# A deformable convolution layer: two of the eight corner weights of a tap move from ScalarE to GpSimd

## The chip, the cores and the metric

The kernel runs on one core of a Trainium2 chip. The core has five engines that work side by side, each through its own queue in order: TensorE (PE, with the weight loads shown apart as PEld), VectorE (DVE), ScalarE (ACT), GpSimd (POOL) and SyncE (SP, which here only issues DMAs). The metric is the time on the device, in microseconds (us), as the median over runs; less is better.

## The reference, cut to what matters

Four layers follow each other on x, an array of 4 images of 128 channels and 128 x 128 pixels, with a group normalisation before and an addition after each: a deformable convolution, a factored dilated convolution, a state space layer with four scans over the image, and a 3 x 3 convolution. The change touches the deformable convolution alone. For each output pixel and each of nine taps an offset is computed from the image, the image is sampled at that fractional position, and a weight matrix is applied:

```python
return corner(y0i, x0i, (1 - ly) * (1 - lx)) + corner(y0i, x0i + 1, (1 - ly) * lx) + corner(y0i + 1, x0i, ly * (1 - lx)) + corner(y0i + 1, x0i + 1, ly * lx)
...
sampled = _bilinear_sample(x, py, px) * mask[:, None]
return jnp.einsum('bckhw,ock->bohw', sampled, weight.reshape(weight.shape[0], C, KK))
```

So a sample is a sum of four corners, each with a weight of its own for every pixel. The first two corners (row `y0`) are called the upper neighbours here, the other two the lower.

## The kernel before, in words

**The main thread and what runs beside it.** The function `scan` writes out the state space layer's four scans, 512 blocks of 16 scan instructions (L1073) on VectorE. Everything else, the deformable layer of the next image included, is written as Python generators that are advanced between scan instructions; `together` sets how far the side work has come for each share of the scans. The order in which the generators are advanced is the order of the instructions on every engine, and `keep_order` makes it final. So when one engine is late, the others find their own work behind the wait that this causes. The first image's deformable layer runs with no scan beside it.

**Which engine does the scan's products.** While a deformable layer runs, the side work announces that GpSimd is busy. The scan then multiplies its states with the output factors on VectorE (L997, the DVE form) instead of GpSimd, and all four input products of a block (L930) are on VectorE as well. GpSimd keeps one 128 x 512 product per block in that time (L902, `steps`), which waits for a copy on ScalarE (L899).

**The deformable layer** (`layer0`). An image has 32 blocks of 4 rows (512 pixels); a block has nine taps, so there are 288 taps in an image and 1152 in all. A table in device memory holds for every position the four corners side by side, 4 x 128 values. A tap goes through these steps:

- `gather` (L447): four indirect DMAs on GpSimd's queue, one for each row of 128 pixels. Rows come in pairs: pair `h` (0 or 1) fills one tile `g` of 128 partitions x 2 rows (`r`) x 4 corners (`c`) x 128 channels. The pool of these tiles has 20 buffers (10 taps) for the first image and 10 buffers (5 taps) for the other three.
- `weigh_upper(h)` (L460): on ScalarE, one instruction on 128 x 128 for each row and upper corner, four for a pair, eight for a tap.
- `weigh_lower(h)` (L473): on VectorE, both lower corners of both rows of a pair in one instruction; its weights `wl` lie in PSUM.
- `turn` (L484): 16 transposing matmuls on TensorE, which add up the four corners in PSUM.
- `copy` (L496, ScalarE), `project` (L504, TensorE, two matmuls), and after the ninth tap `add` (L511, VectorE).

Every 36 taps `positions` works out the indices and weights of the next strip of 16 rows, mostly on VectorE (the indices `idx` at L417).

**The order of a tap's steps** is the list that `weave` reads. Each entry is a delay in taps and a function; at step `t` each function is called for tap `t` less its delay:

```python
order = [[(2, weigh_upper(0)), (2, weigh_lower(0)), (3, turn), (5, project)], [(6, add), (0, gather), (4, copy(True))],
         [(2, weigh_upper(1)), (2, weigh_lower(1))], [(0, look), (3, copy(False))], []]
```

So at one step GpSimd issues the gathers of tap `t`, ScalarE and VectorE weigh tap `t - 2`, and TensorE turns tap `t - 3`. A gather waits until the buffer that it fills is free, that is until the tap five (in the first image ten) before it has been turned.

Of the kernel before, what the change touches and what calls it, by code (L numbers as in the profile page):

```python
# [13 lines left out]
AF = mybir.ActivationFunctionType  # L14
ALU = mybir.AluOpType
# [9 lines left out]
NBLK = H // R  # L25
KK = 9
# [86 lines left out]
def conv_preact_kernel(ctx: ExitStack, tc: tile.TileContext, a: dict, nb: int):  # L113
    nc = tc.nc
# [8 lines left out]
    def load(pool, src, shape, name, **kw):  # L123
        t = pool.tile(shape, F32, name=name, **kw)
        nc.sync.dma_start(t, src)
        return t
# [75 lines left out]
    def blk(t, i):  # L202
        return t[:, i * N : (i + 1) * N]
# [108 lines left out]
    def layer0(st, pairs=10):  # L312
# [5 lines left out]
        with ExitStack() as s:  # L318
# [8 lines left out]
            got = {}  # L327
# [106 lines left out]
            def where(n):  # L434
                i, k = divmod(n, KK)
                return i, k, i // BPS, i % BPS

            def gather(n):
                i, k, j, q = where(n)
                if k == 0:  # L440
                    got["x", i] = load(pp, blk(xb, i), [P, N], "xres", bufs=2)
                idx = got["i", j][1]
                for h in range(2):
                    got["g", n, h] = g = gp.tile([P, 2, 4, P], F32, name="g")
                    for r in range(2):
                        m = ((2 * h + r) * BPS + q) * KK + k
                        nc.gpsimd.indirect_dma_start(  # L447
                            out=g[:, r].rearrange("p q c -> p (q c)"),
                            out_offset=None,
                            in_=table,  # L450
                            in_offset=bass.IndirectOffsetOnAxis(ap=idx[:, m : m + 1], axis=0),
                        )

            def weigh_upper(h):
                def one(n):
                    i, k, j, q = where(n)
                    wv, g = got["i", j][0], got["g", n, h]
                    for r in range(2):
                        for c in range(2):
                            nc.scalar.activation(  # L460
                                g[:, r, c, :], g[:, r, c, :], AF.Copy, scale=wv[:, 2 * h + r, q, k, c : c + 1]
                            )

                return one

# [72 lines left out]
            for n, _ in enumerate(positions(0)):  # L538
                yield share * min(1.0, (n + 1) / 21)
            order = [[(2, weigh_upper(0)), (2, weigh_lower(0)), (3, turn), (5, project)], [(6, add), (0, gather), (4, copy(True))],  # L540
                     [(2, weigh_upper(1)), (2, weigh_lower(1))], [(0, look), (3, copy(False))], []]
            while st["rows"] <= NBLK:
# [841 lines left out]
    def head(b):  # L1384
        st = sts[b]
        table = [(loads(None, layer0_table(st), True), 12)] if b < 2 else []
        return table + [(loads("POOL", layer0(st)), 28), (loads("PE", layer1(st), True), 14),
                (loads("PE", layer2_pre(st), True), 36)]
# [11 lines left out]
    for f in layer0(sts[0], 20):  # L1400
        tick()
        for _ in range(3):
            next(ahead, None)
            tick()
# [103 lines left out]
```

## Time and profile before

| | |
|---|---|
| median of 3 runs | 20775.48 us (20770.23 to 20790.63) |
| the profiled execution, its own time | 20873.01 us, 0.47% above that median |
| its span, first to last instruction | 20871.2 us |
| busy DVE / POOL / PE / ACT | 16828.5 / 15930.9 / 15906.6 / 13184.7 us |
| indirect gathers L447 on POOL | 4608, mean 1043 ns, busy 4807.6 us |
| upper weights L460 on ACT | 9216, mean 392 ns, busy 2897.4 us |
| first image's gathers (stage A) | from 215 to 1933 us of the span, no scan beside |
| second, third, fourth image's (stages B, C, D) | 3449 to 5328, 8650 to 10450, 13548 to 15369 us, with scans |

How to read the profile: all times count from the first instruction of the span. A row of a group gives line, engine, operation, what it writes and reads, and the count; behind the bar its busy time in us and the mean ns of one; behind the second bar the idle time of the engine just before these instructions, and who ended most of it. "issue" means that nothing the profile shows was waited for. Busy time of neighbouring instructions can overlap, so that 9216 instructions of 392 ns fill 2897.4 us, not 3613.

### The profile page before, as it was taken

To read this page: it belongs to the slowest core of one execution; us is meant where nothing else is said; L and a number is where in the kernel's file an instruction comes from. 1 tells how busy PE (TensorE), PEld (TensorE's weight loads), DVE (VectorE), ACT (ScalarE), POOL (GpSimd) and SP (SyncE) were. 2 spreads that over 40 slices of the span, in tenths; PEclk is the share of its full clock that TensorE was granted. 3 is DMA by queue.
4 is the path that set the end of the run, shared out by engine and by line. 5 is a ranking of instruction groups with operands and counts; after the bars stand their busy time and mean duration, and the time that the engine had idled before them with its cause. 6 is when DMAs were issued, how large, how long until landed. Compare 5 with 4: busy or idle time off the path is not lost.

```text
span 20871.2 us, 208527 instructions
## 1 busy us (share of the span) xinstructions
PE 15906.6 (76%) x58778; PEld 6786.0 (33%) x58778; DVE 16828.5 (81%) x14665; ACT 13184.7 (63%) x26230; POOL 15930.9 (76%) x9453
## 2 busy tenths in 40 slices
PE   4667776777878888777788887877777877677778
PEld 2444222444322223344422222344432222222223
DVE  1222588888999999878799889978889998999983
ACT  3444566677666666666667776666666767655563
POOL 3664577666788888777668888866768889999994
PEclk7878888889989999889889999988888988899899
DMA  7666678777767777777777796777776777555673
GB/s 234 191 193 190 193 228 284 248 255 252 246 206 226 231 237 254 236 253 255 247 232 226 224 249 230 255 240 246 252 237 218 235 215 220 185 185 193 199 219 120
DMA packets 2909344, 4717.42 MB, mean 226 GB/s; under 512 B 1095248, under 2 KB 1369240, under 8 KB 2831264
## 3 DMA queue, kind: packets, MB, share of 16 engines
q1 hardware_dynamic: 2539552, 3495.83, 52.3%
q0 software_dynamic: 368640, 1208.25, 18.5%
q8 instruction: 476, 7.80, 0.1%
q14 instruction: 676, 5.54, 0.1%
HBM read 3766.27 MB, written 908.60 MB: 224 GB/s over the span
## 4 chain that ended last, share of the span: by engine, by line
DVE 35%; PE 21%; issue 11%; ACT 11%; DMA 9%; another core or an unknown queue 5%; POOL 3%; SPq 3%; DVEq 0%; POOLq 0%; ACTq 0%
DVE h L1073 20%; DVE h L930 11%; PE pst L484 5%; PE psum L895 4%; DMA du<-stepsd 3%; ACT pa L960 3%; ACT g L460 3%; PE acc L504 2%; DVE g L473 2%; PE dub L923 2%; DMA delta<-stepsd 2%; PE yacc L971 2%; PE p L1303 1%; DMA g<-table,idx 1%
## 5 line engine op out<-in xcount | busy, mean ns | idle before, releaser
L1073 DVE TENSOR_TENSOR_SCAN h<-pa,carry,h 128x512 f32<-128x512 f32 x8192 | 10010.0, 1268 | 811.5 <-ACT pa L960 582.9
L960 ACT ACTIVATE pa<-delta,neg_a 128x512 f32<-128x512 f32 x8192 | 5535.9, 686 | 4528.0 <-DVE h L1073 3464.9
L997 POOL TENSOR_TENSOR h<-h,cb 128x2048 f32<-128x2048 f32 x1692 | 7670.8, 4534 | 136.3 <-POOL carry L991 0.4
L447 POOL DMA_INDIRECT g<-table,idx x4608 | 4807.6, 1043 | 2454.1 <-issue 1523.6
L930 DVE TENSOR_TENSOR h<-du,dub 128x2048 f32<-128x2048 f32 x1625 | 3688.0, 2270 | 961.8 <-PE dub L923 294.7
L484 PE MATMUL pst<-ident,g 128*128 128x128 f32 x18432 | 2693.6, 303 | 1242.6 <-issue 516.0
L923 PE MATMUL dub<-u,xb_sb 128*128 128x512 f32 x3250 | 2073.1, 724 | 1843.3 <-DVE h L930 1532.3
L484 PEld LDWEIGHTS pst<-ident,g 128*128 128x128 f32 x18432 | 2377.9, 158 | 2230.3 <-issue 1139.0
L460 ACT ACTIVATE g<-g,wt 128x128 f32<-128x128 f32 x9216 | 2897.4, 392 | 50.8 <-DMA g<-table,idx 47.6
L971 PE MATMUL yacc<-h,gather_sb 128*32 128x512 f32 x16384 | 2375.6, 644 | 108.9 <-POOL h L997 63.8
L930 POOL TENSOR_TENSOR h<-du,bb 128x2048 f32<-128x2048 f32 x423 | 1927.7, 4557 | 16.5 <-DMA du<-stepsd 16.5
L496 ACT COPY smp<-pst 128x512 f32<-128x512 f32 x1152 | 664.7, 577 | 1749.8 <-remote 1175.9
L473 DVE TENSOR_TENSOR g<-g,wl 128x512 f32<-128x512 f32 x2304 | 1485.7, 671 | 194.3 <-issue 108.5
L504 PE MATMUL acc<-smp,w_sb 128*128 128x512 f32 x2304 | 1355.3, 670 | 307.7 <-DVE x L511 162.8
L923 PEld LDWEIGHTS dub<-u,xb_sb 128*128 128x128 f32 x3250 | 600.3, 213 | 3025.2 <-DVE h L930 2200.9
L902 POOL TENSOR_TENSOR steps<-steps,u 128x512 f32<-128x512 f32 x512 | 652.9, 1275 | 1095.3 <-ACT steps L899 1080.0
L1303 PE MATMUL p<-xn,w_l_sb 128*128 128x508 f32 (+2 forms) x2304 | 1148.6, 620 | 1.8 <-ACT xn L1282 1.8
L971 PEld LDWEIGHTS yacc<-h,gather_sb 128*32 128x32 f32 x16384 | 343.5, 111 | 1886.3 <-issue 1349.6
L895 PE MATMUL psum<-e,ident 128*128 128x512 f32 x1024 | 607.1, 677 | 387.7 <-ACT bc L889 348.5
L511 DVE TENSOR_TENSOR x<-acc,xres 128x512 f32<-128x512 f32 x128 | 87.5, 684 | 967.5 <-remote 500.4
L895 PE MATMUL psum<-one_e,less 128*128 128x512 f32 x1024 | 629.2, 701 | 297.3 <-ACT one_e L891 296.5
L997 DVE TENSOR_TENSOR h<-h,cb 128x2048 f32<-128x2048 f32 x356 | 816.6, 2294 | 12.1
(169 smaller groups left out, 17288.9 us busy)
## 6 DMA issues: line engine op xcount, KB each, us to landing
cb<-bcd SPq DMA_DIRECT2D x512, 1024.0 KB
delta<-stepsd SPq DMA_DIRECT2D x2048, 256.0 KB
du<-stepsd SPq DMA_DIRECT2D x2048, 256.0 KB
stepsd<-steps SPq DMA_DIRECT2D x512, 512.0 KB
table<-gt SPq DMA_DIRECT2D x512, 256.0 KB
bb<-bcd SPq DMA_DIRECT2D x512, 256.0 KB
win<-nd SPq DMA_DIRECT2D x512, 160.0 KB
g<-table,idx POOLq DMA_INDIRECT x4608
```

The costliest lines, as they stand in the source:

```text
L447: nc.gpsimd.indirect_dma_start(out=g[:, r].rearrange("p q c -> p (q c)"), out_offset=None, in_=table, in_offset=bass.IndirectOffsetOnAxis( ...
L460: nc.scalar.activation(g[:, r, c, :], g[:, r, c, :], AF.Copy, scale=wv[:, 2 * h + r, q, k, c : c + 1])
L473: nc.vector.tensor_mul(g, g, wl.unsqueeze(3).to_broadcast([P, 2, 2, P]))
L484: nc.tensor.matmul(pst[:, r * P : (r + 1) * P], g[:, r % 2, q, :], ident, start=q == 0, stop=q == 3, is_transpose=True,)
L504: nc.tensor.matmul(got["a", i], w0[:, k, :], got.pop(("c", n)), start=k == 0, stop=k == KK - 1)
L895: nc.tensor.matmul(pd, sign, t, start=n == 0, stop=n == 3)
L923: nc.tensor.matmul(p, xb[:, seq[t][1], j, :], c["u"], start=True, stop=True)
L930: engine.tensor_mul(h, c["du"], b.unsqueeze(1).to_broadcast([P, NG, N]))
L960: nc.scalar.activation(pa, blocks[t]["d", g], AF.Exp, scale=neg_a[:, k, at : at + 1])
L971: nc.tensor.matmul(c["y"][g * Q : (g + 1) * Q, :], gather, c["h", j][:, g, :], start=j == 0, stop=last and not second,)
L997: engine.tensor_mul(h, h, c["cb"][:, j, :].unsqueeze(1).to_broadcast([P, NG, N]))
L1073: nc.vector.tensor_tensor_scan(o, f, o, carry[:, n : n + 1], ALU.mult, ALU.add)
```

## The change

In `gather`, behind the two indirect DMAs of a pair, GpSimd now multiplies one slice of an older tile: row 1, upper corner 1 of the same pair of the tap two before. ScalarE leaves that slice out. For the last two taps of an image, which no later gather follows, ScalarE does it as before. A small function `neighbour` returns the slice and the column of its weights.

```diff
                             in_offset=bass.IndirectOffsetOnAxis(ap=idx[:, m : m + 1], axis=0),
                         )
+                    if n >= 2:
+                        g, w = neighbour(n - 2, h, 1, 1)
+                        nc.gpsimd.tensor_scalar(g, g, w, None, ALU.mult)
+
+            def neighbour(n, h, r, c):
+                i, k, j, q = where(n)
+                return got["g", n, h][:, r, c, :], got["i", j][0][:, 2 * h + r, q, k, c : c + 1]
 
             def weigh_upper(h):
                 def one(n):
-                    i, k, j, q = where(n)
-                    wv, g = got["i", j][0], got["g", n, h]
                     for r in range(2):
                         for c in range(2):
-                            nc.scalar.activation(
-                                g[:, r, c, :], g[:, r, c, :], AF.Copy, scale=wv[:, 2 * h + r, q, k, c : c + 1]
-                            )
+                            if r == 1 and c == 1 and n + 2 < NBLK * KK:
+                                continue
+                            g, w = neighbour(n, h, r, c)
+                            nc.scalar.activation(g, g, AF.Copy, scale=w)
 
                 return one
```

## The prediction

> **What bounds the kernel now.** I began with the page's busy shares and slices.
>
> ```profile
> PE 15906.6 (76%) x58778; PEld 6786.0 (33%) x58778; DVE 16828.5 (81%) x14665; ACT 13184.7 (63%) x26230; POOL 15930.9 (76%) x9453
> ...
> ACT  3444566677666666666667776666666767655563
> POOL 3664577666788888777668888866768889999994
> ```
>
> No engine is full over the whole span, and ACT, which the change relieves, is the least busy of the four. The change acts in four stages only, so next comes the view that sums busy time by stretch, one row for each image's gathers (A, B, C, D).
>
> ```profile
> core 0: us, PE busy (x) PEld busy (x) DVE busy (x) ACT busy (x) POOL busy (x), PEclk, DMA share, GB/s
> 215.00:1933.00 1718.00, 1027.82 (x5584) 739.58 (x5585) 431.75 (x751) 819.54 (x2544) 1092.56 (x1152) 0.79 0.64 191
> 3449.00:5328.00 1879.00, 1466.84 (x7298) 823.19 (x7297) 1624.06 (x1646) 1297.91 (x3361) 1278.93 (x1184) 0.89 0.75 251
> 8650.00:10450.00 1800.00, 1370.82 (x6979) 797.55 (x6980) 1416.38 (x1488) 1207.83 (x3210) 1268.62 (x1178) 0.88 0.76 248
> 13548.00:15369.00 1821.00, 1369.97 (x6968) 795.96 (x6968) 1416.11 (x1486) 1208.36 (x3210) 1274.69 (x1178) 0.87 0.75 245
> ```
>
> By busy time POOL looks two thirds full (1274.7 of 1821 in D). The timeline of POOL in stage B, and of VectorE beside it, says otherwise:
>
> ```profile
> 4371.64 0.95 POOL L447 DMA_INDIRECT g<-table,idx  x1 [0.30 <-issue]
> 4374.77 0.95 POOL L447 DMA_INDIRECT g<-table,idx  x1 [2.19 <-ACT smp L496]
> 4376.02 0.95 POOL L447 DMA_INDIRECT g<-table,idx  x1 [0.30 <-issue]
> 4377.15 1.28 POOL L902 TENSOR_TENSOR steps<-steps,u 128x512 f32<-128x512 f32 x1 [0.18 <-ACT steps L899]
> 4378.58 0.98 POOL L447 DMA_INDIRECT g<-table,idx  x1
> ```
>
> ```profile
> 4372.35 2.29 DVE L997 TENSOR_TENSOR h<-h,cb 128x2048 f32<-128x2048 f32 x1
> ```
>
> Two things are to be seen. A gather shows 0.95 us but the next starts 1.25 us later: 0.30 us belong to it and to nothing that is waited for. And the gap of 2.19 us spans VectorE's L997 to 0.13 us past its end (4374.64): ScalarE's copy is named, but the gather was held by that product. So POOL's occupied time is busy time, plus 0.30 us for each of 1152 gathers (346 us), plus the gaps over an L997 (read off the timeline: 0, 121, 30 and 28 us). That makes 1438 of 1718 us in A, 1746 of 1879 in B, 1644 of 1800 in C and 1649 of 1821 in D. In B to D POOL is the fullest engine (91 to 93%); VectorE has 86, 79 and 78%. The stage's first gather also waits about 30 us for its indices (34.5, 30 and 31). What is left for POOL to give is 280, 98, 126 and 141 us.
>
> Last, the chain of waits in stages A and B:
>
> ```profile
> by line: another core or an unknown queue 37.3%; PE pst L484 16.8%; ACT g L460 13.8%; issue 12.2%; PE acc L504 7.9%; ACT smp L496 2.6%; DVE g L473 2.5%; POOL g L447 2.2%; DMA g<-table,idx 2.0%; PE po L359 1.3%; DVE x L511 0.3%; PE ptp L366
> by line: issue 20.8%; DVE h L1073 10.1%; PE pst L484 9.3%; DVE h L930 8.0%; DVE g L473 7.5%; ACT g L460 7.1%; another core or an unknown queue 6.3%; DMA g<-table,idx 4.3%; PE acc L504 4.1%; PE dub L923 3.2%; ACT pa L960 2.6%; POOL g L447 2.
> ```
>
> The upper weights L460 are 13.8% of the chain in A and 7.1% in B (5.9 and 6.3% in C and D). No single engine carries it.
>
> **The change, part by part.**
>
> *Removed from ACT.* Each image loses 286 x 2 = 572 of 2304 weighings. Eight take 2.45 us in a row, 0.306 us each: 175 us of ACT per image. On the path lies at most a quarter of L460's share of the chain: 1718 x 13.8% / 4 = 59 us in A, 33, 27 and 29 us in B, C, D. Where POOL sets the pace none of it counts, so I take it in A alone.
>
> *Added to POOL.* 572 multiplications of 128 x 128 by a column, per image. The trace has no such instruction. Its rows give a line: L997 on POOL, 2048 elements, 4534 ns; L902, 512 elements, 1275 ns; so 2.12 ns an element and 189 ns fixed, and L991, a copy of 4 elements, takes 195 ns as the line says. At 128 elements that is 0.46 us. L902 stood between two gathers at the cost of 4378.58 - 4376.02 - 1.25 = 1.31 us, of which 0.18 was a wait: 0.15 us less than its own 1.28, because it takes over part of the 0.30. So one scale costs POOL 0.46 - 0.15 = 0.31 us, an image 572 x 0.31 = 177 us. Lower end: L991's 195 ns, 0.05 us net, 26 us an image. Upper end: L902 itself, 1.28 us, 645 us an image; but it reads two tensors four times as long, so for the range I use the line plus the fixed part once more for the column of weights, 0.65 us: 0.50 net, 286 us an image. I take the middle because it lies on the line of three rows.
>
> The Trainium skill ("GPSIMD Engine Reference", section 4.1) speaks against the change: plain elementwise work belongs on VectorE, and GpSimd is about half as fast with two inputs, which L997 confirms (4534 against 2294 ns). The same row calls GpSimd roughly line-rate with one input. By that and its 1.2 GHz, as an estimate, a scale would take 0.107 + 0.189 = 0.30 us, net 0.15, and an image 86 us; no run here shows it.
>
> *Waits that move.* The scale waits for gathers issued two taps earlier, at least eight gathers or 10 us. Each gather ends with 16 packets of 4 bytes; their order gives landing at a median of 3.3 us after issue in A and 4.0 to 4.2 in B to D, 99% within 8.6. So that wait is nothing; were it not, the next pair's gathers would queue behind it. The pair h = 1 now stands behind the scale of h = 0 in POOL's queue, and L902 behind both. No DMA and nothing on SP moves. TensorE's turn now also waits for POOL, for a scale behind the gathers of two taps on. Counting gathers issued when a turn starts, POOL is 8.0 taps ahead in A and 3.5 to 3.75 in B to D (medians); three are needed, and 4% or fewer have less. A turn that waits holds TensorE's scan products behind it and VectorE behind those.
>
> *The shared path with VectorE.* L997 holds gathers already, as seen; the scales wait in the same 2.3 us, not in new ones. The other way round, a scale is running 2 x 0.46 / 6.4 = 14% of the time and would hold L997 for 0.23 us on average: 334 x 0.14 x 0.23 = 11 us in all, which I leave out.
>
> The skill ("SBUF — State Buffer", section "Who interferes with whom") says a VectorE instruction with two SBUF inputs contends with a GpSimd instruction that reads SBUF, but infers that such a tensor_tensor leaves descriptor generation alone. The gap of 2.19 us disagrees for these indexed gathers. By the inference POOL would have had 121 us more to give in B; the sum goes by the gap.
>
> *Sum.* Of what POOL has left, I let the scales use half, since the rest is tied to waits at fixed places (L902 for L899, strip ends). B: 177 - 49 = 128. C: 177 - 63 = 114. D: 177 - 71 = 106. A: 177 - 140 - 59 = -22; but there TensorE's hold-ups in "an unknown queue" set the pace, which I can't price, so I take 0, between -59 and +177. Sum 348 us. The profiled execution would go from 20873 to 21221; carried over to the median, 0.47% lower, 20775 + 348 = 21123, rounded 21120 (+1.7%).
>
> **The rivals.**
>
> *1. GpSimd has room, ACT's relief counts (faster).* Speaks for it: gathers wait for ACT by name, POOL's busy time is 76%. Against: most of those gaps lie over L997 or are the 0.30 us. It decides if a scale's net cost is under 98/572 = 0.17 us in B, 0.22 in C, 0.25 in D, that is under some 0.32 us of duration. Then the quarters of L460 are the gain: 59 + 33 + 27 + 29 = 148 us, 20627.
>
> *2. The scale is dear.* At 0.65 us: 286 less the same halves, 237 + 223 + 215 = 675, and in A 286 - 140 - 59 = 87. Sum 762, 21540. For it: the column operand, which no row has.
>
> *3. A new wait takes over.* Once POOL sets the pace, ACT, VectorE and TensorE catch up, and turns stand at the three-tap limit waiting for the scale. If one turn in ten then waits for half a tap of gathers (2.5 us), that is 29 x 2.5 = 72 us a stage, 215 in three, on top of the forecast: 21340. Against: a turn is due two taps (10 us) before its buffer is wanted.
>
> *4. Nothing moves:* only if a scale's cost equals what POOL has left.
>
> **How the numbers follow.** The forecast has 0.47 (21000 to 21260), rival 1 0.16, rival 2 0.17, rival 3 0.15, rival 4 0.05. About 0.2% (42 us) is what a measurement of this kernel tells from no change. Of rival 1 some 0.03 falls within it: faster 0.13, same 0.08, slower 0.79. The range leaves out most of rival 1 and rival 2's end: 20700 to 21500.
>
> **What would show it.** A new POOL row, 2288 scales, near 0.46 us; L460 at 6928. POOL's occupied share in B to D at 97% or more, the stages at about 2000, 1910 and 1925 us, A near 1718. Under rival 1 the stages shrink and POOL stays near 95%; under rival 3 "PE pst L484 <- POOL g" stands among the longest waits. I am wrong if the scale's row is far from 0.46, if its own wait is on a DMA, or if stage A moves by more than 100 us.

## The result, and the profile after

The changed kernel takes 21419.07 us (median of 4 runs, 21407.09 to 21436.96) against 20772.85 us before on the same chip: a ratio of 1.0306, 95% interval 1.0294 to 1.0318. That is 646 us slower, where the forecast had 348 us. 21419 lies within its range of 20700 to 21500, though outside the 21000 to 21260 to which it gave its chance of 0.47. The profiled execution of the changed kernel has a span of 21435.2 us and is compared with the span of before, 20871.2 us: 564 us more.

In the changed file the gather is still L447; the new product on GpSimd is L455, ScalarE's weighing L468 (was L460), VectorE's L479, the turn L490, ScalarE's copy L502, GpSimd's `steps` L908 and the product by the output factors L1003 (was L997). The page of the changed kernel, busy shares and slices, answers to the first view shown of before:

```profile
PE 16207.9 (76%) x58778; PEld 6768.2 (32%) x58778; DVE 16921.0 (79%) x14665; ACT 12642.1 (59%) x23942; POOL 17673.4 (82%) x11741
...
ACT  3444565555667766555566776655556767665563
POOL 4886577888788888888878888888878889999994
```

ScalarE lost 543 us of busy time, GpSimd gained 1743. The stretches of the four stages (their gathers, as before; same columns):

```profile
215.00:2001.00 1786.00, 1171.68 (x5671) 751.64 (x5671) 486.13 (x763) 717.87 (x2027) 1490.88 (x1723) 0.83 0.63 184
3511.00:5551.00 2040.00, 1524.21 (x7314) 825.87 (x7313) 1650.23 (x1655) 1152.05 (x2806) 1746.65 (x1755) 0.87 0.72 232
8862.00:10859.00 1997.00, 1447.98 (x7011) 794.45 (x7011) 1443.38 (x1497) 1082.03 (x2666) 1703.81 (x1749) 0.87 0.71 225
13947.00:15947.00 2000.00, 1443.96 (x7011) 793.87 (x7011) 1445.51 (x1500) 1081.70 (x2665) 1706.31 (x1750) 0.87 0.71 224
```

From first gather to last, A is 66 us longer (1784 against 1718), B 161 (2040 against 1879), C 198 and D 178: 603 us, where the two spans differ by 564: the whole loss lies in these four stages. POOL's timeline in stage D shows what fills them:

```profile
15005.67 0.62 POOL L455 TENSOR_SCALAR g<-g,wt 128x128 f32<-128x128 f32 x1
15006.46 1.01 POOL L447 DMA_INDIRECT g<-table,idx  x1 [0.17 <-POOL g L455]
15007.78 0.94 POOL L447 DMA_INDIRECT g<-table,idx  x1 [0.30 <-PE acc L510]
15008.75 0.63 POOL L455 TENSOR_SCALAR g<-g,wt 128x128 f32<-128x128 f32 x1
15009.56 1.01 POOL L447 DMA_INDIRECT g<-table,idx  x1 [0.17 <-POOL g L455]
```

The gap between two gathers is 0.30 us as it always was, 0.17 us behind a scale and 0.03 us ahead of one. Behind the stage's first gather no gap of POOL is longer than 0.34 us in any of the four stages. Before, longer gaps held 269, 241, 176 and 192 us beyond their first 0.34 us each; this sum is called POOL's waiting from here on. POOL is now occupied from end to end. A pair of gathers with its scale takes 3.10 us from start to start (median of 2200), a pair without one 2.50 us in before (median of 4432): a scale costs 0.60 us of POOL, 343 us in an image.

The groups of POOL and ACT, first as they were before (L447 and L460), then in the changed kernel:

```profile
L447 POOL DMA_INDIRECT g<-table,idx x4608 | 4807.6, 1043 | 2454.1 <-issue 1523.6 <-DMA xres<-in_x_dram 214.2 <-ACT smp L496 175.7
L460 ACT ACTIVATE g<-g,wt 128x128 f32<-128x128 f32 x9216 | 2897.4, 392 | 50.8 <-DMA g<-table,idx 47.6
```

```profile
L447 POOL DMA_INDIRECT g<-table,idx x4608 | 4949.3, 1074 | 1409.3 <-issue 496.7 <-POOL g L455 350.0 <-DMA xres<-in_x_dram 215.4
...
L455 POOL TENSOR_SCALAR g<-g,wt 128x128 f32<-128x128 f32 x2288 | 1597.6, 698 | 77.3
```

```profile
L468 ACT ACTIVATE g<-g,wt 128x128 f32<-128x128 f32 x6928 | 2295.3, 393 | 659.4 <-DMA g<-table,idx 617.1 <-issue 27.5 <-POOL g L455 6.8
```

The waits of the changed kernel (what waits, for what, us in total, times, longest us):

```profile
PEld pst L490 <- POOL g L455: 2412.1, 1442, 7.3
...
PE pst L490 <- POOL g L455: 2044.1, 1339, 6.9
DVE g L479 <- DMA g<-table,idx: 1590.7, 775, 7.2
```

The scale takes 0.62 us (median 622 ns; the mean of 698 holds 86 long ones of 1.8 us and more, all of them over a VectorE L1003). No group of idle time on POOL is put down to the scale's own wait for data. Everything downstream now waits for POOL: ScalarE and VectorE for gathers that have not landed, TensorE's turn for the scale.

### The profile page after: what moved, and what is told of

The parts are those of the page before. It is cut to its first block, busy times and chain, and to the rows that moved or that the text cites. A ratio compares the mean times of both kernels' runs of the same rounds, so it can differ in the third digit from the quotient of the medians.

```text
span 21435.2 us, 211218 instructions
## 1 busy us (share of the span) xinstructions
PE 16207.9 (76%) x58778; PEld 6768.2 (32%) x58778; DVE 16921.0 (79%) x14665; ACT 12642.1 (59%) x23942; POOL 17673.4 (82%) x11741
## 5 line engine op out<-in xcount | busy, mean ns | idle before, releaser
L1003 POOL TENSOR_TENSOR h<-h,cb 128x2048 f32<-128x2048 f32 x1692 | 7674.2, 4536 | 136.9 <-POOL carry L997 1.0
L447 POOL DMA_INDIRECT g<-table,idx x4608 | 4949.3, 1074 | 1409.3 <-issue 496.7
L490 PE MATMUL pst<-ident,g 128*128 128x128 f32 x18432 | 2901.8, 304 | 2126.7 <-POOL g L455 2044.1
L490 PEld LDWEIGHTS pst<-ident,g 128*128 128x128 f32 x18432 | 2311.9, 156 | 3415.8 <-POOL g L455 2412.1
L479 DVE TENSOR_TENSOR g<-g,wl 128x512 f32<-128x512 f32 x2304 | 1533.1, 674 | 1778.9 <-DMA g<-table,idx 1590.7
L468 ACT ACTIVATE g<-g,wt 128x128 f32<-128x128 f32 x6928 | 2295.3, 393 | 659.4 <-DMA g<-table,idx 617.1
L455 POOL TENSOR_SCALAR g<-g,wt 128x128 f32<-128x128 f32 x2288 | 1597.6, 698 | 77.3
L502 ACT COPY smp<-pst 128x512 f32<-128x512 f32 x1152 | 668.7, 581 | 1569.9 <-PE acc L510 1449.1
L510 PE MATMUL acc<-smp,w_sb 128*128 128x512 f32 x2304 | 1491.1, 735 | 25.4 <-DVE x L517 24.4
L908 POOL TENSOR_TENSOR steps<-steps,u 128x512 f32<-128x512 f32 x512 | 653.7, 1277 | 906.6 <-ACT steps L905 904.6
L1003 DVE TENSOR_TENSOR h<-h,cb 128x2048 f32<-128x2048 f32 x356 | 821.3, 2307 | 12.2
```

What stands on the lines that cost most here:

```text
L447: nc.gpsimd.indirect_dma_start(out=g[:, r].rearrange("p q c -> p (q c)"), out_offset=None, in_=table, in_offset=bass.IndirectOffsetOnAxis( ...
L455: nc.gpsimd.tensor_scalar(g, g, w, None, ALU.mult)
L468: nc.scalar.activation(g, g, AF.Copy, scale=w)
L479: nc.vector.tensor_mul(g, g, wl.unsqueeze(3).to_broadcast([P, 2, 2, P]))
L490: nc.tensor.matmul(pst[:, r * P : (r + 1) * P], g[:, r % 2, q, :], ident, start=q == 0, stop=q == 3, is_transpose=True,)
L510: nc.tensor.matmul(got["a", i], w0[:, k, :], got.pop(("c", n)), start=k == 0, stop=k == KK - 1)
```

## The experiments

The first theory after the result: **POOL's time** is the loss. A stage takes its old length or POOL's occupied time, whichever is longer, and 572 scales of 0.60 us net push the occupied time over the old length. The rival: **the new wait**. TensorE's turn waits 2412 us for POOL's scale in the view above, and that chain (gather two taps on, scale, turn) sets the pace. A second question is why the scale costs what it does, and a third what ScalarE's relief is worth. Runs of one group share one chip and the runs of the kernel before on it: 20858.91 us for the spare tile, the corner left out, the one pair and the buffers; 20769.86 for the three quarters, the wait alone (two kernels) and the prices; 20782.94 for the form of two tiles, where it fits and the one pair run again. The last run had a chip of its own. In the kernels with a scratch tile the lines are shifted by one or a few.

**The scale on a tile that nobody reads.**

```diff
-                        nc.gpsimd.tensor_scalar(g, g, w, None, ALU.mult)
+                        nc.gpsimd.tensor_scalar(spare, ident, w, None, ALU.mult)
...
-                            if r == 1 and c == 1 and n + 2 < NBLK * KK:
-                                continue
```

> ScalarE weighs all eight upper corners again; GpSimd does the same 2288 multiplications, behind the same gathers and with the same column of weights, but from a constant into a scratch tile that nothing reads. So GpSimd's time stays and the wait for its result is gone. Theory 1 (GpSimd's own time is the loss: 0.60 us for each multiplication, 343 us an image, GpSimd without a pause in all four stages): about the changed kernel's 21419 us, between 21350 and 21500, and GpSimd again without waits. Theory 2 (the wait of TensorE's turn for GpSimd, three taps instead of five, is the loss): near the 20773 us of the kernel before, at most 20900.

Measured: 21393.95 us, ratio 1.0262 (1.0245 to 1.0279). The turns have nothing to wait for on POOL, and most of the loss is there. In us it is 25 below the changed kernel's first runs; the ratio is lower because the kernel before is slower on this chip. Its stages are 1782, 2031, 1989 and 1988 us, within 12 us of the changed kernel's, with no idle time on POOL.

**The corner left out.**

```diff
-                    if n >= 2:
-                        g, w = neighbour(n - 2, h, 1, 1)
-                        nc.gpsimd.tensor_scalar(g, g, w, None, ALU.mult)
```

> One upper corner of each pair is left out altogether: ScalarE weighs three, GpSimd none (the last two taps of an image as before). Theory 1: ScalarE's relief is worth little where GpSimd is the fullest engine: 20700 to 20780 us. Rival (ScalarE's share of the chain counts): a quarter of that share in the four stages, 148 us, 20625 us or less.

Measured: 20814.3 us, 0.9981 (0.9972 to 0.9991). ScalarE's relief by itself is worth 45 us, little more than two chips differ by (see the one pair below): its stages are 1710, 1864, 1800 and 1799 us against 1718, 1879, 1799 and 1821.

**One pair only.**

```diff
-                    if n >= 2:
+                    if n >= 2 and h == 1:
...
-                            if r == 1 and c == 1 and n + 2 < NBLK * KK:
+                            if h == 1 and r == 1 and c == 1 and n + 2 < NBLK * KK:
```

> Only the second pair of a tap has its corner weighed on GpSimd, 286 an image instead of 572; ScalarE does the first pair's. Theory 1: GpSimd gets 172 us an image. What it had left in the four stages was 280, 98, 126 and 141 us, so the first image's stage stays, and the other three grow by 74, 46 and 31 us: 20925 us, between 20850 and 21000. Theory 2 (any wait for GpSimd brings the three-tap limit): most of the 646 us are back, 21200 or more.

Measured: 20824.56 us, 0.9983 (0.9973 to 0.9992). Half of the scales cost nothing, where a proportional cost would have been 320 us. POOL's waiting has gone from 269, 241, 176 and 192 us to 88, 0, 8 and 6: the scales used the whole of the room in B to D. My rule that only half of it could be used is wrong. The expected 20925 missed too, though it let the scales use all of the 98, 126 and 141 us that I had reckoned for B to D: there was more room than that. The kernel stands at the edge.

The same kernel was run again later on another chip:

> The kernel in which GpSimd weighs the corner of the second pair alone, once more in five rounds, beside the kernel before: whether half of the products is really a little faster, or the same. GpSimd is filled and no more in the last three stages, so both theories: 0.997 to 1.000.

Measured: 20784.16 us, 1.0000 (0.9991 to 1.0009). So the gain of the first time isn't a property of the kernel that can be relied on; between two chips the ratio moved by 0.17%, and the relief of 0.19% above is no surer than that.

**Fewer buffers in the first image.**

```diff
-        layer0(sts[0], 20)
+        layer0(sts[0], 10)
```

> The kernel before, with 10 instead of 20 buffers for the first image's gathered tiles, nothing else. In the kernel before, ScalarE's copy waited 1176 us in all for something that the profile does not name, in stage A above all, with gathers up to ten taps ahead; in the changed kernel, whose gathers keep about two and a half taps ahead of the turns, that wait is gone. Theory a (the hold-ups come from gathers that run far ahead): stage A goes from 1718 us towards the 1440 us of the gathers alone, 20500 to 20700 us. Theory b (the hold-ups have another cause and the buffers only bridge them): stage A is the same or longer, 20770 to 20950 us.

Measured, on the kernel before with this edit: 20858.41 us, 1.0003 (0.9994 to 1.0013). In before, some of ScalarE's copies start long after the transposes that they read have ended (in stage A 90 of 288, by a median of 9.8 us), and the trace names what released them only as "remote". Halving the buffers left it as it was: 693 us in stage A before, 728 in this kernel. For the whole span (before, then this kernel):

```profile
ACT smp L496 <- remote: 1175.9, 219, 34.3
```

```profile
ACT smp L496 <- remote: 1210.3, 213, 17.6
```

In the changed kernel no wait of this kind is left, on any engine. What it is was not found; it doesn't depend on these buffers.

**Three quarters of the scales**, to see whether the cost sets in at the edge.

```diff
-                    if n >= 2:
+                    if n >= 2 and (h == 1 or n % 2 == 0):
```

(The condition of ScalarE's `continue` changes with it.)

> GpSimd weighs the corner for both pairs in every second tap and for the second pair alone in the others: 429 scales an image, where the change has 572 and the kernel with one pair has 286. If GpSimd's occupied time bounds a stage as soon as its idle time is used up, and the kernel with one pair stands just at that point, the stages are those of the changed kernel less 143 times 0.60 to 0.65 us: some 1695 in the first, which then stays at before's 1718, and 1950, 1910 and 1910 in the others, together 270 us over before, ratio 1.013. If each scale costs the same wherever it stands, three quarters of the change's loss: 480 us, 1.023. If what costs is something that sets in only with the last scales (the turns that wait for GpSimd in every tap), under 1.005.

Measured: 21049.07 us, 1.0134 (1.0118 to 1.0151), the first theory's 1.013. The stages by gathers were expected at 1718, 1950, 1910 and 1910 us and came out at 1698, 1947, 1902 and 1902.

```profile
218.00:1915.00 1697.00, 1125.13 (x5671) 737.10 (x5671) 483.51 (x762) 759.38 (x2168) 1389.81 (x1580) 0.84 0.67 193
3415.00:5362.00 1947.00, 1466.02 (x7314) 800.52 (x7313) 1644.27 (x1653) 1191.49 (x2949) 1639.73 (x1613) 0.90 0.76 243
8666.00:10567.00 1901.00, 1393.78 (x7011) 779.88 (x7011) 1444.99 (x1497) 1116.23 (x2806) 1593.58 (x1606) 0.88 0.74 236
13660.00:15561.00 1901.00, 1392.01 (x7011) 778.71 (x7011) 1442.43 (x1498) 1115.50 (x2801) 1593.71 (x1606) 0.89 0.75 236
```

Each row loses 101 to 113 us of POOL's busy time against the changed kernel's, and 89 to 99 us of its length, where 143 scales of 0.60 us are 86: where POOL is the bound, the stage follows it.

**The wait alone.** The changed kernel and one that differs only in whose data the scale touches, side by side. In the second nobody weighs that corner.

```diff
-                        nc.gpsimd.tensor_scalar(g, g, w, None, ALU.mult)
+                        nc.gpsimd.tensor_scalar(spare, ident, w, None, ALU.mult)
```

> GpSimd does its product from the identity into a scratch tile that nobody reads, ScalarE weighs the other three, and nobody weighs that one corner: the work on each engine is the change's, without the wait of the transposes for GpSimd's product. If the wait costs nothing, the ratio is the changed kernel's, 1.031 within 0.002. If it costs what the changed kernel had over the scratch tile with all eight on ScalarE, 1.026 or less.

> The changed kernel itself, so that it stands beside the others against the same runs of the kernel before. Both theories: 1.031 within 0.002.

Measured: 21393.25 us, 1.0302 (1.0285 to 1.0319) without the wait; 21413.23 us, 1.0308 (1.0291 to 1.0325) with it. The difference of 0.0006, 20 us between the medians, is within either interval. So the turn's wait is not what the 643 us are made of. Without it other waits took its place (waits of the kernel without the scale's wait):

```profile
ACT g L469 <- DMA g<-table,idx: 2658.9, 2465, 23.8
DVE g L480 <- DMA g<-table,idx: 2438.9, 1250, 8.1
```

All of them are waits for the same late engine: POOL issues gathers as fast as it can, and what hangs on a gather waits, whichever semaphore comes last.

**What a product costs on GpSimd.** ScalarE weighs all eight; behind each pair one of four forms goes into the scratch tile, by tap.

```diff
+                        if n % 4 == 0:
+                            nc.gpsimd.tensor_scalar(spare, ident, w, None, ALU.mult)
+                        elif n % 4 == 1:
+                            nc.gpsimd.tensor_scalar(spare[:, 0:64], ident[:, 0:64], w, None, ALU.mult)
+                        elif n % 4 == 2:
+                            nc.gpsimd.tensor_scalar(spare, ident, 0.5, None, ALU.mult)
+                        else:
+                            nc.gpsimd.tensor_copy(spare, ident)
```

> ScalarE weighs all eight neighbours again. Behind each pair of gathers GpSimd runs one instruction from the identity into a scratch tile that nobody reads, its form going round with the tap: the product with a column on 128 elements, the same on 64, the product with a constant on 128, a plain copy on 128. If the scale's 0.62 us is the price of reading its factor from a column, the form with a constant and the copy take about 0.46 us, the row of three rows. If it is the price of f32 elements on this engine, all three forms on 128 take about 0.62 and the one on 64 elements between 0.31 (nothing fixed) and 0.46 (half of it fixed). The time follows the mean price: with the means of 0.62, 0.40, 0.46 and 0.46, 0.14 us less per instruction than the change's own form, 78 us a stage that GpSimd fills, so near 1.015 of before; with 0.62, 0.40, 0.62 and 0.62, near 1.022.

Measured: 21035.39 us (one run), 1.013 of before. The four forms among POOL's groups:

```profile
L457 POOL TENSOR_SCALAR spare<-ident,wt 128x128 f32<-128x128 f32 x568 | 432.3, 761 | 22.0
L461 POOL TENSOR_SCALAR spare<-ident 128x128 f32<-128x128 f32 x576 | 370.6, 643 | 15.4
...
L459 POOL TENSOR_SCALAR spare<-ident,wt 128x64 f32<-128x64 f32 x568 | 324.9, 572 | 18.7
L463 POOL COPY spare<-ident 128x128 f32<-128x128 f32 x576 | 218.8, 380 | 2.7
```

The means hold the instructions that were stopped beside VectorE; the medians are 622, 558, 463 and 297 ns. Neither expectation was right. The column costs 64 ns, not 160. The two widths give 2.5 ns an element and some 304 ns fixed for the form with a scalar, against 2.12 and 189 on my line; the copy takes less than half. So it is the form of the instruction that sets the price.

**The same product in the form that the line was drawn through.** My line went through two products of two tiles, L997 and L902, and L991, a copy of four elements, lay on it.

```diff
-                        nc.gpsimd.tensor_scalar(g, g, w, None, ALU.mult)
+                        nc.gpsimd.tensor_mul(g, g, w.to_broadcast([P, P]))
```

> The change with its product written as a product of two tiles, the weight's column broadcast along the row, in place of the product with a scalar column. The three rows that the forecast drew its line through were products of two tiles (4534 ns for 2048 elements, 1275 for 512); if the line holds for that form at 128 elements, the new rows show 0.46 us instead of the 0.62 of the change, 0.16 us less for each of 572 in four images, 92 us a stage while GpSimd stays filled: about 1.0308 less 366 of 20770, so 1.013. If a short product costs what the scalar form does, 1.031. If reading two operands or the broadcast costs more on short rows, above 1.031. The turns wait for GpSimd here as in the change.

Measured: 20842.81 us, 1.0032 (1.0020 to 1.0044). The same work in another form takes back nine tenths of the loss. The product's row (duration min/median/max) and its timeline in stage D:

```profile
L455 POOL TENSOR_TENSOR g<-g,wt x2288: 407/409/2552, 229.0 to 15360.9; 128x128 f32<-128x128 f32 x191
```

```profile
15002.57 0.42 POOL L455 TENSOR_TENSOR g<-g,wt 128x128 f32<-128x128 f32 x1
15003.14 0.98 POOL L447 DMA_INDIRECT g<-table,idx  x1 [0.16 <-POOL g L455]
15004.43 0.95 POOL L447 DMA_INDIRECT g<-table,idx  x1 [0.30 <-issue]
15005.40 0.41 POOL L455 TENSOR_TENSOR g<-g,wt 128x128 f32<-128x128 f32 x1
```

0.41 us, a little under the line's 0.46, and 2.83 us for a pair with it: 0.33 us net, the forecast's 0.31. It did better than the expected 1.013 because that sum took off 0.16 us a product, where the net price fell by 0.27. The stages are 1686, 1876, 1839 and 1836 us, with 45, 0, 1 and 1 us of waiting on POOL: full, and hardly over the edge.

**Where it fits.** The form of two tiles, for the second pair alone, and in the first image, whose stage had most room, for the first pair of every second tap as well.

```diff
-                    if n >= 2:
+                    if n >= 2 and (h == 1 or pairs == 20 and n % 2 == 0):
...
-                            if r == 1 and c == 1 and n + 2 < NBLK * KK:
+                            if (h == 1 or pairs == 20 and n % 2 == 0) and r == 1 and c == 1 and n + 2 < NBLK * KK:
```

> GpSimd weighs the corner of the second pair alone, and in the first image, whose stage had the most idle time, also of the first pair in every second tap; written as a product of two tiles. If a product costs 0.46 us, GpSimd has some 45 us left in each stage of the last three images, and the first stage takes 1690 to 1700: 20 to 60 us less than before, 0.997 to 0.999. If it costs 0.62 or more, the stages of the kernel with one pair and the first stage of the one with three quarters: 0.998 to 1.000, and above 1.000 only if the product costs over 0.65.

Measured: 20709.61 us, 0.9967 (0.9957 to 0.9978), in the same group as the two runs of 1.0000 and 1.0032. By the ratios it beats the kernel before by 0.33% and the changed one by 3.3%. POOL keeps 98, 52, 36 and 40 us of waiting in stages of 1693, 1829, 1764 and 1775 us. All four are shorter than those of the kernel without the corner, in which ScalarE is relieved of more and POOL of everything; that run was on another chip, but it raises the question of what the gain comes from.

**Relief, or a slower pace of gathers?** The same products at the same places on the scratch tile, with ScalarE weighing all eight.

```diff
-                        nc.gpsimd.tensor_mul(g, g, w.to_broadcast([P, P]))
+                        nc.gpsimd.tensor_mul(spare, ident, w.to_broadcast([P, P]))
```

> The same products at the same places as where they fit (second pair, and in the first image every second tap's first pair), but from the identity into a scratch tile that nobody reads, with ScalarE weighing all eight neighbours. If the 0.33% of the kernel where they fit comes from ScalarE's relief, it is gone: 1.000 to 1.002, since GpSimd still has some 40 us of idle time a stage. If it comes from the gathers' slower pace (a product between two pairs spreads them), it stays: 0.996 to 0.998.

Measured: 20453.56 us against 20081.66 us of the kernel before, 1.0182 (1.0168 to 1.0196). Neither expectation holds, and the run doesn't answer the question, for it went to a chip on which the kernel before is over 3% faster than on the others (its granted clock is 0.904 there, 0.889 on the chip of the run above). Its stretches:

```profile
216.00:1797.00 1581.00, 1066.98 (x5694) 698.42 (x5694) 482.64 (x762) 920.82 (x2597) 1284.71 (x1581) 0.88 0.70 208
3303.00:5096.00 1793.00, 1424.62 (x7322) 812.34 (x7321) 1653.17 (x1656) 1307.35 (x3381) 1472.27 (x1470) 0.90 0.79 264
8405.00:10146.00 1741.00, 1357.16 (x7016) 787.31 (x7016) 1445.40 (x1497) 1232.80 (x3229) 1424.96 (x1463) 0.89 0.79 257
13231.00:14969.00 1738.00, 1360.58 (x7016) 787.69 (x7016) 1447.64 (x1498) 1233.85 (x3228) 1422.34 (x1463) 0.89 0.79 258
```

The products are the same and cost the same (409 to 412 ns), but POOL has 0, 6, 2 and 1 us of waiting, and the stages are as long as its occupied time. By the net price of 0.33 us the added products come to 429 x 0.33 + 3 x 286 x 0.33 = 425 us; 372 were measured. That fits a kernel before in which, on that chip, POOL had next to no room: the room that the others had would then be time in which TensorE was held up. There is no profile of before from that chip, so this is argued and not shown, and whether the gain where it fits comes from ScalarE or from the pace stays open.

## Why the prediction was right, and where it was wrong

**POOL sets the pace: right.** The prediction's occupied times, read as busy time plus 0.30 us a gather plus the gaps over L997, carry the stages of three kernels once the net price is the measured one (0.60 from the changed kernel, 0.33 from the product of two tiles). Old occupied time plus scales times net price, against the measured stage, in us:

| run | scales an image, net us | A | B | C | D |
|---|---|---|---|---|---|
| change | 572 x 0.60 | 1781 / 1784 | 2089 / 2040 | 1987 / 1998 | 1992 / 2000 |
| three quarters | 429 x 0.60 | 1695 / 1698 | 2003 / 1947 | 1901 / 1902 | 1906 / 1902 |
| product of two tiles | 572 x 0.33 | 1627 / 1686 | 1935 / 1876 | 1833 / 1839 | 1838 / 1836 |

A, C and D are met within 11 us wherever POOL is full; in A with the cheap form it isn't (1686, near the old 1718). B comes out 49 to 59 us too long each time. The reason lies in the 121 us that I put down to L997 there: in the trace of before, B's gaps of more than 0.34 us lie beside an L997 for only 62 us (23 in C, 18 in D), so the rest of the 121 can have been room. With these in place of 121, 30 and 28 us, B comes to 2031, 1945 and 1876, and C and D stay within 18 us.

**"So one scale costs POOL 0.46 - 0.15 = 0.31 us": wrong, and it is the step that failed.** The scale measured 0.62 us where I had 0.46, and 0.60 net where I had 0.31. The two long rows behind the line were products of two tiles, and the change issues a product with a scalar column, a form that no row of the trace had. For the form of the rows the step is good (0.41 and 0.33). The upper end of the range's price, 0.65 us, was nearest for a wrong reason: it added the fixed 189 ns for the column, and the column costs 64. The 0.15 us taken off for the 0.30 behind a gather is wrong for this form too: of the 0.30, 0.03 and 0.17 us stay as gaps ahead of and behind the scale, and the gather behind it lasts 1.01 us in place of 0.95.

On the Trainium skill ("GPSIMD Engine Reference", section 4.1): the estimate of 0.30 us that I had made from its rate for one input is met by the copy's 297 ns, and missed twofold by the product with a column at 622. The class of a page's rule has to be read as narrowly as a row's.

**"I let the scales use half": wrong, and the room was mis-sized too.** The scales used all of the room: 241, 176 and 192 us of waiting went to zero in B to D, and half of the scales cost nothing. And the 98, 126 and 141 us of room were too few: I had taken off the 34.5, 30 and 31 us that a stage's first gather waits for its indices, but that wait ends where the stage begins (at 3449.3 us in B) and isn't part of its 1879, 1800 and 1821 us. With the right price and the wrong half the sum would have been 343 - 49 = 294 in B, 280 in C, 272 in D and 343 - 140 - 59 = 144 in A, 990 us in all. With the whole room and the wrong price it would have been 177 - 98, 177 - 126 and 177 - 141, that is 79, 51 and 36, 166 us in all. With the price, the half and the first gather's wait put right, the first row of the table less the old lengths, 63 + 210 + 187 + 171 = 631 us, against 603 measured in the stages. The errors of price and half went against each other, so that 348 stands nearer to the 646 than either correction alone would have brought it. That 21419 lies in the range owes as much to this luck as to the working.

**Stage A: within its bound.** I took 0 between -59 and +177; it is +66 us. There, too, POOL became the bound: 1784 us measured, 1781 occupied. So the ground on which I took 0, that TensorE's hold-ups set the pace there, went with the change: 693 us of ScalarE's copies waiting for "remote" in A became none.

**The waits that move.** The scale's own wait for its gathers is nothing, as said. Turns start 2.25 to 2.5 taps of gathers behind POOL's front now (median), where it was some 8 in A and 3.5 to 3.75 in the others. Under "the shared path" I wrote that the scales wait in the same 2.3 us as the gathers and left them out: 86 of 2288 were stopped by VectorE's L1003, for 157 us in all beyond their 0.62 us each. That is partly time that gathers had lost there before (the gaps beside L997 above).

That agrees with the skill's page "SBUF — State Buffer", section "Who interferes with whom": an instruction of VectorE with two inputs in SBUF contends with one of GpSimd that reads SBUF. L1003 reads two such inputs; each of the 86 long scales lies over it and ends 0.4 to 0.5 us behind its end.

**Rival 1** is out for the change as a whole: the relief alone is 0.2% at most, 45 us by the one run that has it, where the quarters of L460 made 148. **Rival 2**, the dear scale, is what happened as to the price; its total of 762 kept the same halves, and its 21540 stands nearer to the 21419 than the forecast's 21120. **Rival 3** is instructive: its sign came true to the letter, "PE pst <- POOL g" stands for 2044 us and the weight loads of the same transposes for 2412, the second longest wait of the kernel, and still it costs next to nothing (1.0302 without, 1.0308 with). The sign was a bad one, since an engine that sets the pace is waited for by everything behind it.

## What to carry to other kernels

Before work goes to an engine whose busy share looks low, count what it is occupied: here each gather hid 0.30 us behind its 0.95, and a POOL at 68 to 70% by its busy time in B to D was some 90% taken. Up to that room added work is nearly free, above it every 0.1 us counts in full, so a change of this kind is a matter of how much, and a smaller dose can win (0.9967, on one chip) where the whole one loses (1.0308). And take the price from a row of the same form of instruction: the same product cost 0.62 us with a scalar column and 0.41 us with a broadcast tile, and the form alone was worth some 580 us here (643 us over the kernel before against 60, each in its group of runs).

## What the hardware showed that I had not expected

- On GpSimd, 128 x 128 f32: product with a scalar column 622 ns, with a constant 558, product of two tiles with the column broadcast 409, copy 297. Two inputs are cheaper than one and a scalar.
- The waits put down to "remote" (1175.9 us for ScalarE's copy alone in before) all but go when POOL has at most 6 us of waiting in any of the four stages (ScalarE's copies then wait 0 to 87 us so, in the change and five other kernels), and are there with 1136.0 us where POOL has 36 to 98 us of waiting a stage. With the product of two tiles they are there in A (752 us; POOL waits 45) and nearly gone in B to D (1, 43 and 45 us). They don't depend on the first image's buffers. What they are stays open.
- The kernel before took 20770 to 20859 us on four groups of runs and 20082 us on one further chip. There products of the cheap form, without the relief of ScalarE, cost 1.8%, at places where another chip, with the relief, had room for them. So a verdict on a change that lives in an engine's spare time may hold for the chip that it was measured on.
